# A sixteenth of layer 3's exponentials moved to VectorE, and the four attentions run as one stream

## The chip, the cores and the metric

The kernel runs on one core of a Trainium2 chip. A core has five engines, each with its own instruction stream that it works through in order: TensorE (PE, matrix products; its weight loads are listed as PEld), ScalarE (ACT, activations such as the exponential), VectorE (DVE, element-wise work), GpSimd (POOL) and SyncE (SP, which issues most DMAs). They meet through semaphores. The metric is the device time of one execution in microseconds. The kernel before takes 4205.69 us (median of three runs, 4199.02 to 4210.75).

## The reference, cut to what matters

Four layers follow each other on an input of 2 x 128 x 64 x 64, each of the form `x = x + layer(group_norm(x))`. Layer 3 is softmax attention over all 4096 positions, with 8 heads of 16 channels:

```python
q, k, v = proj(wq, bq), proj(wk, bk), proj(wv, bv)      # (B, 8, 16, 4096)
a = jnp.einsum('bhcq,bhck->bhqk', q, k) / jnp.sqrt(128.)
a = jax.nn.softmax(a, axis=-1)
o = jnp.einsum('bhqk,bhck->bhcq', a, v)
x = x + o.reshape(B, C, h, w)
```

Layer 0 has, among much else, one softmax attention with 4 heads of 32 channels over the same 4096 positions. Both attentions skip the maximum of the softmax (a bound on the scores is checked, with a general version behind it) and so need, for each score, one exponential, one product with the values, and a share in a sum.

## The kernel before, in words

The layers run one after the other. Everything in layers 0 and 3 is issued in the order of the program on each engine: `_in_order` ties each instruction to the one before it on its engine, so nothing is rearranged by a scheduler.

**Layer 3.** Each of the 2 batch entries has 2 groups of 4 heads, so there are four attentions. An attention takes its 4096 queries in 8 blocks of 512 (`qb`), and for each block its 4096 keys in 32 tiles of 128 (`kt`): 1024 iterations in all. One iteration does this:

- `scores` (L2102): 8 matmuls into two PSUM tiles `ps_s` of 128 x 1024, called here pair 0 and pair 1 (heads 0 and 1, heads 2 and 3). Query and key are each split in two parts, so each head has two matmuls that add up; all first parts are issued (two for pair 0, two for pair 1), then all second parts.
- two activations (L2112), one for each pair: the exponential of 128 x 1024 scores from PSUM to a `weights` tile in SBUF.
- `multiply` (L2121) for the iteration two before this one: 4 matmuls (8 records in the trace) that add weights times values to one accumulator `ps_acc`. Beside the values, `vt` holds a column block of ones, so the sum for the softmax is accumulated in the same product.

PSUM is full: the pool `f3_sp` has three tiles for scores and `f3_acc` two of half that size. Since an iteration takes two of three score tiles in rotation, pair 0 of an iteration reuses the tile of pair 1 two iterations before, and pair 1 reuses the tile of pair 0 of the iteration just before.

After the last key tile of a block, `done` divides by the sum: five DVE operations (L2143 to L2148; the reciprocal L2146 takes 128 x 512 elements), and four DMAs write the rows out.

The side work prepares the next attention while one runs: queries and keys (L2030 to L2046), values (L2056, L2063), the bound (L2076 to L2091), the statistics of the next batch entry. It is a generator that is advanced after the iterations kt = 4, 12 and 20 of each block. Its matmuls go between two iterations on TensorE. In the first block of the first attention it is advanced before every even iteration, since its keys and values are only just being made. Each attention ends by draining its last two `multiply` before the next starts.

**Layer 0's attention** (L1343, L1352, L1760, L1800) has the same tiling. There the softmax's sum is made otherwise: DVE adds the weights of several iterations (128 x 2048 elements each), and TensorE then reduces the result with a matrix of ones (4 matmuls). `SUMMED` says how many iterations go in one such group: 7, 6, 7, 6 and 6 of the 32.

Of the kernel before, what the change touches and what calls it, by code (L numbers as in the profile page):

```python
# [17 lines left out]
S = H * W  # L18
CH = 512
# [1268 lines left out]
SUMMED = (7, 6, 7, 6, 6)  # L1288
F32R = mybir.dt.float32r
ENGINES = (  # L1290
# [672 lines left out]
def _layer3(ctx, tc, X, l3, cst, out, worst, here):  # L1963
# [6 lines left out]
    pp = ctx.enter_context(tc.tile_pool(name="f3_p", bufs=8))  # L1970
# [16 lines left out]
    def folded(b, got):  # L1987

        x = X[:, b, :]
        if b:  # L1990
            mean, rstd = _group_stats_pow(nc, two, acc, x, cst, mhalf)
        else:
            mean, rstd = here[:, 0:1], here[:, 1:2]
        yield
# [24 lines left out]
    def queries_and_keys(b, t, f, q, k, idle):  # L2019

        wqk, _, bqk, _ = f
        bq, bk, bk2 = (bqk[:, n, t : t + 1] for n in range(3))
        for c in range(NCH):
            cols = slice(c * CH, (c + 1) * CH)
            ps = acc()
            nc.tensor.matmul(ps, wqk[:, t, :], X[:, b, cols], start=True, stop=True)  # L2030

            qq = two.tile([128, CH], F32, tag="qq", name="qq", bufs=1)
            nc.vector.stream_shuffle(qq, ps, OF_Q)  # L2033
            kk = two.tile([128, CH], F32, tag="kk", name="kk", bufs=1)
            nc.vector.stream_shuffle(kk, ps, OF_K)  # L2035
            hi = two.tile([128, CH], F32R, tag="hi", name="hi", bufs=1)
            if c < idle:
                nc.scalar.activation(hi, kk, AF.Identity, bias=bk)
                nc.scalar.activation(kk, kk, AF.Identity, bias=bk2, scale=upper)
                nc.scalar.activation(q[0][:, cols], qq, AF.Identity, bias=bq)  # L2040
            else:
                nc.vector.tensor_scalar_add(hi, kk, bk)
                nc.vector.tensor_scalar(kk, kk, bk, upper, ALU.add, ALU.mult)
                nc.vector.tensor_scalar_add(q[0][:, cols], qq, bq)
            nc.vector.scalar_tensor_tensor(k[:, cols], hi, sign, kk, ALU.mult, ALU.add)
            nc.vector.scalar_tensor_tensor(  # L2046
                q[1][:, cols], qq, bq, q[0][:, cols], ALU.add, ALU.subtract
            )
            yield
# [20 lines left out]
    def bound(b, t, q, k):  # L2070


        top = two.tile([128, 2, 2], F32, tag="top", name="top")
        for n, x in enumerate((q[0], k)):
            for i in range(2):
                nc.vector.tensor_reduce(  # L2076
                    top[:, n, i : i + 1],
                    x[:, i * S // 2 : (i + 1) * S // 2],
                    AX.X,
                    ALU.max,  # L2080
                    apply_absolute_value=True,
                )
                yield
        m = two.tile([128, 2], F32, tag="m", name="m")
        nc.vector.tensor_reduce(m, top, AX.X, ALU.max)
        mm = two.tile([128, 1], F32, tag="mm", name="mm")
        nc.vector.scalar_tensor_tensor(mm, m[:, 0:1], lower, m[:, 1:2], ALU.mult, ALU.mult)
        ps = acc()
        nc.tensor.matmul(ps[:, 0:1], head_sum, mm, start=True, stop=True)
        n = 1 + 2 * b + t  # L2090
        nc.vector.tensor_scalar_mul(worst[:, n : n + 1], ps[:, 0:1], 1.02)  # L2091
        yield

    def attend(b, t, q, k, vt, early):
        ac = [None]

        def scores(qb, kt):
            ps = [spp.tile([128, 2, CH], F32, tag="sp", name="ps_s") for _ in range(2)]
            for n in range(2):
                for j in range(4):  # L2100
                    rows = slice(32 * j, 32 * j + 32)
                    nc.tensor.matmul(  # L2102
                        ps[j // 2][:, j % 2, :],
                        k[rows, kt * 128 : (kt + 1) * 128],
                        q[n][rows, qb * CH : (qb + 1) * CH],
                        start=(n == 0),
                        stop=(n == 1),
                    )
            w = []
            for p in range(2):  # L2110
                w.append(pp.tile([128, 2, CH], F32, tag="weights", name="weights"))
                nc.scalar.activation(w[p], ps[p], AF.Exp)  # L2112
            return w

        def multiply(qb, kt, w):
            if kt == 0:
                ac[0] = acc()
            for j in range(4):

                i = j % 2  # L2120
                nc.tensor.matmul(  # L2121
                    ac[0][32 * j : 32 * j + 32, :],
                    vt[:, kt, j // 2, i : i + 2, :].rearrange("p a d -> p (a d)"),
                    w[j // 2][:, i, :],
                    start=(kt == 0),
                    stop=(kt == NQT - 1),
                )
            if kt == NQT - 1:
                done(qb, ac[0])

        def done(qb, ps):
            cols = slice(qb * CH, (qb + 1) * CH)

            places = [
                (slice(32 * j + 16 * (j % 2), 32 * j + 16 * (j % 2) + 16),
                 slice(64 * t + 16 * j, 64 * t + 16 * j + 16))
                for j in range(4)
            ]
            xs = residual[qb % 2]
            for to, rows in places:  # L2140
                nc.sync.dma_start(xs[to, :], X[rows, b, cols])
            u = two.tile([128, CH], F32, tag="u", name="u", bufs=1)
            nc.vector.tensor_copy(u, ps)  # L2143
            r = two.tile([128, CH], F32, tag="r", name="r", bufs=1)
            nc.vector.stream_shuffle(r, u, [(i + 16) % 32 for i in range(32)])  # L2145
            nc.vector.reciprocal(r, r)  # L2146
            nc.vector.tensor_mul(u, u, r)  # L2147
            nc.vector.tensor_add(u, u, xs)  # L2148
            for at, rows in places:
                nc.sync.dma_start(out[b, rows, cols], u[at, :])  # L2150

        waiting = []
        for qb in range(NCH):
            for kt in range(NQT):
                if kt % 2 == 0:
                    over = next(early, early) is early
                waiting.append((qb, kt, scores(qb, kt)))
                if len(waiting) > 2:
                    multiply(*waiting.pop(0))
                yield kt if over else None  # L2160
        for x in waiting:
            multiply(*x)
# [10 lines left out]
    def work():  # L2173

        for b in range(B):
            f = []
            yield from folded(b, f)
            for t in range(2):
                first = b == 0 and t == 0
# [12 lines left out]
                else:  # L2192
                    for _ in early:
                        yield
# [155 lines left out]
```

## Time and profile before

One profiled execution took 4197.72 us; its span, from first to last instruction, is 4195.9 us. The median of the timed runs is 8 us above the former.

| stretch of the profiled execution | us |
|---|---|
| layer 0's two attentions, first to last exponential (L1352) | 193 to 803 and 1003 to 1590 |
| layer 3's attention, start of the first to start of the last exponential (L2112) | 2234.3 to 4179.7 |
| end of the span | 4195.9 |
| ACT busy with L2112 | 1884.8 (2048 instructions) |
| ACT idle before L2112 | 62.8 |
| granted TensorE clock, mean | 0.985 |

In a line of the profile, the operation is followed by what it writes and reads, its shape and count; after the bar stand the busy time in us, the mean duration of one in ns, and the idle time of the engine before these instructions with what ended it. Instructions of one engine overlap, so the busy time over the count is closer to the pace than the mean duration is.

### The profile page before, as it was taken

How to read it: one execution, taken by the hardware profiler on the slowest of the kernel's cores; microseconds unless marked ns; L12 is line 12 of the kernel's file. 1: busy time of each engine (PE TensorE's matmuls, PEld its weight loads, DVE VectorE, ACT ScalarE, POOL GpSimd, SP SyncE). 2: the span in 40 equal slices, each digit the busy share in tenths (PEclk: the TensorE clock that was granted, in tenths of full speed). 3: DMA queues.
4: the chain of work that ended last, by engine and by line, in shares of the span. 5: the costliest groups of instructions: out<-in, count | busy, mean ns of one | idle time of the engine just before them, and what ended most of it. 6: DMA issues, size and time to landing. Idle time of an engine off the chain costs nothing. (4 is left out here: it accounts for less than half of the span.)

```text
span 4195.9 us, 90633 instructions
## 1 busy us (share of the span) xinstructions
PE 4026.9 (96%) x40014; PEld 1494.0 (36%) x40014; DVE 2127.8 (51%) x2374; ACT 3332.9 (79%) x4035; POOL 71.3 (2%) x145
## 2 busy tenths in 40 slices
PE   7999999989999998997999999999999999999998
PEld 4522222354222224445664333333333333333332
DVE  4678888657888888986754112221132102211111
ACT  4478888735888883326647999999999999999998
POOL 1001000010000001000000000000000000000000
PEclk9999999999999999998999999999999999999999
DMA  1199960000000000004750000000000000000000
GB/s 49 29 188 182 179 90 1 2 2 2 2 1 2 2 1 12 1 1 171 290 208 4 6 6 6 4 6 6 4 6 6 6 4 6 6 4 6 6 6 5
DMA packets 158855, 159.40 MB, mean 38 GB/s; under 512 B 24809, under 2 KB 148713, under 8 KB 154354
## 3 DMA queue, kind: packets, MB, share of 16 engines
q1 hardware_dynamic: 158450, 153.50, 15.7%
q8 instruction: 315, 5.16, 0.5%
q14 instruction: 90, 0.74, 0.1%
HBM read 145.09 MB, written 73.40 MB: 52 GB/s over the span
## 5 line engine op out<-in xcount | busy, mean ns | idle before, releaser
L2112 ACT ACTIVATE weights<-ps_s 128x1024 f32<-128x1024 f32 x2048 | 1884.8, 1099 | 62.8 <-PE ps_s L2102 62.3
L1352 ACT ACTIVATE weights<-ps_s 128x1024 f32<-128x1024 f32 x1024 | 992.9, 1023 | 180.6 <-PE ps_s L1343 164.2
L2121 PE MATMUL ps_acc<-weights,vt 128*32 128x512 f32 x8192 | 1092.8, 605 | 0.0
L2102 PE MATMUL ps_s<-q,k 32*128 32x512 f32 x8192 | 924.9, 444 | 5.4 <-ACT weights L2112 5.4
L1800 DVE TENSOR_TENSOR sums<-sums,weights 128x2048 f32<-128x2048 f32 x352 | 806.7, 2292 | 38.4 <-ACT weights L1352 5.2
L2102 PEld LDWEIGHTS ps_s<-q,k 32*128 32x128 f32 x8192 | 471.2, 182 | 839.4 <-ACT weights L2112 773.6
L1343 PE MATMUL ps_s<-q,k 32*64 32x512 f32 x8192 | 627.3, 613 | 7.1 <-ACT weights L1352 2.4
L1760 PE MATMUL ps_acc<-weights,vt 128*32 128x512 f32 x4096 | 550.9, 606 | 6.6 <-ACT weights L1352 3.6
L2143 DVE COPY u<-ps_acc 128x512 f32<-128x512 f32 x32 | 22.1, 691 | 1039.0 <-PE ps_acc L2121 1039.0
L1343 PEld LDWEIGHTS ps_s<-q,k 32*64 32x64 f32 x8192 | 159.6, 130 | 436.4 <-PE ps_s L1343 320.3
L2121 PEld LDWEIGHTS ps_acc<-weights,vt 128*32 128x32 f32 x8192 | 162.9, 108 | 379.2 <-issue 367.2
L1800 DVE TENSOR_TENSOR sums<-weights 128x2048 f32<-128x2048 f32 x80 | 183.3, 2291 | 113.6 <-ACT weights L1352 113.6
L1760 PEld LDWEIGHTS ps_acc<-weights,vt 128*32 128x32 f32 x4096 | 81.2, 108 | 426.3 <-issue 403.3
L662 DVE SCALAR_TENSOR_TENSOR X<-g,w,X 128x2048 f32<-128x2048 f32 x84 | 197.4, 2350 | 2.6
L1548 PE MATMUL ps_sp<-pad,diag 32*32 32x512 f32 x4608 | 158.9, 597 | 2.3 <-ACT q L1568 1.3
L1008 PE MATMUL ps_z<-w_ri,e 128*32 128x128 f32 x2048 | 137.3, 408 | 14.3 <-DVE e L950 12.1
L2063 DVE TENSOR_TENSOR vt<-ps_acc,bv 128x384 f32<-128x384 f32 x32 | 17.8, 557 | 246.0 <-PE ps_acc L2056 246.0
L1548 PEld LDWEIGHTS ps_sp<-pad,diag 32*32 32x32 f32 x4608 | 95.0, 103 | 54.2 <-issue 15.9
L2033 DVE LOAD_MASK_SELECT qq<-ps_acc x32 | 0.4, 14 | 222.6 <-PE ps_acc L2030 222.6
L2146 DVE RECIPROCAL r<-r 128x512 f32<-128x512 f32 x32 | 107.3, 3353 | 1.1
L950 DVE TENSOR_SCALAR e<-ps_pe 32x136 f32<-32x136 f32 (+1 forms) x352 | 104.4, 297 | 4.9
L948 ACT ACTIVATE e<-ps_pe 32x136 f32<-32x136 f32 (+1 forms) x352 | 99.2, 282 | 4.1
(289 smaller groups left out, 2552.5 us busy)
## 6 DMA issues: line engine op xcount, KB each, us to landing
w_ri<-w_r SPq DMA_DIRECT2D x16, 2112.0 KB, 8.2
w_ri<-w_i SPq DMA_DIRECT2D x16, 2112.0 KB, 13.5
w_r<-in_L_conv_kr_w SPq DMA_DIRECT2D x15, 528.0 KB, 13.5
w_r<-in_L_conv_kr_x SPq DMA_DIRECT2D x15, 528.0 KB, 13.3
w_r<-in_L_conv_kr_y SPq DMA_DIRECT2D x15, 528.0 KB, 13.0
w_r<-in_L_conv_kr_z SPq DMA_DIRECT2D x15, 528.0 KB, 13.2
w_i<-in_L_conv_ki_w SPq DMA_DIRECT2D x15, 528.0 KB, 13.8
w_i<-in_L_conv_ki_x SPq DMA_DIRECT2D x15, 528.0 KB, 12.7
```

The costliest lines, as they stand in the source:

```text
L662: nc.vector.scalar_tensor_tensor(xi, g[:, i : i + H // 2, j : j + W], w8[:, s : s + 1], xi, ALU.mult, ALU.add)
L950: nc.vector.tensor_scalar_mul(out, got[of, :, s], sign)
L1008: nc.tensor.matmul(out.rearrange("p (n f o) -> p n f o", n=2, f=2), e[:, s, 2 * j : 2 * j + 2, :].rearrange("p f x -> p (f x)"), w.rearran ...
L1343: nc.tensor.matmul(ps[j // 2][to, j % 2, :], k[rows, kt * 128 + 64 * half : kt * 128 + 64 * half + 64], q[rows, qb * CH : (qb + 1) * CH], ...
L1352: nc.scalar.activation(w[:, 2 * p : 2 * p + 2, :], ps[p], AF.Exp)
L1548: nc.tensor.matmul(ps[r // 2][to, r % 2, :].rearrange("p (h w) -> p h w", w=W), diag[rows, grp, t, :], pad[rows, y0 : y0 + ROWS, t % 3 : t ...
L1760: nc.tensor.matmul(ac[n][rows, :], lhs(rows), w[:, j, :], start=first, stop=last)
L1800: nc.vector.tensor_add(parts[0].rearrange("p j c -> p (j c)"), t.rearrange("p j c -> p (j c)"), w.rearrange("p j c -> p (j c)"),)
L2102: nc.tensor.matmul(ps[j // 2][:, j % 2, :], k[rows, kt * 128 : (kt + 1) * 128], q[n][rows, qb * CH : (qb + 1) * CH], start=(n == 0), stop= ...
L2112: nc.scalar.activation(w[p], ps[p], AF.Exp)
L2121: nc.tensor.matmul(ac[0][32 * j : 32 * j + 32, :], vt[:, kt, j // 2, i : i + 2, :].rearrange("p a d -> p (a d)"), w[j // 2][:, i, :], star ...
L2146: nc.vector.reciprocal(r, r)
```

## The change

In layer 3, four of the 64 exponentials of a block are taken from ACT and computed on DVE: pair 0 of the key tiles 4 and 18, pair 1 of 11 and 25. DVE scales and converts a score to an integer, whose bits are taken apart into an exponent and a mantissa, evaluates a polynomial in the mantissa, and multiplies by the power of two: eight instructions on 128 x 1024 elements, where the first reads PSUM and so gives the score tile back. The first is issued with the scores, the others in six steps, one before each following iteration. The finished weights are multiplied later, in the places 10, 17, 24 and 31 of the order of products (`ORDER`). `LAG` is now 3 iterations instead of 2, and there are 12 tiles for weights instead of 8.

Queries are kept in a tile for each block of 512 rather than one for all. The side work is cut into smaller steps and placed after the iterations in `SIDE`: a block of keys and queries is spread over four of them (only the first has a matmul), and values, bound and statistics use the others. The maxima for the bound are taken with each block of keys (128 x 512) rather than later over 128 x 2048. `done` transposes the accumulator, takes four reciprocals of 32 x 16 elements, multiplies, and transposes back. The four attentions share one list of products that wait, so that none drains before the next.

In layer 0, `SUMMED` becomes four groups of eight.

```diff
-SUMMED = (7, 6, 7, 6, 6)
+SUMMED = (8, 8, 8, 8)
...
+LAG = 3
+SIDE = (6, 9, 13, 16, 20, 23, 27, 30)
+BY_VECTOR = {(4, 0): 10, (11, 1): 17, (18, 0): 24, (25, 1): 31}
...
-    pp = ctx.enter_context(tc.tile_pool(name="f3_p", bufs=8))
+    pp = ctx.enter_context(tc.tile_pool(name="f3_p", bufs=12))
     spp = ctx.enter_context(tc.tile_pool(name="f3_sp", bufs=3, space=PSUM))
...
+    def exponentials(ps, out):
+        i = two.tile([128, 2 * CH], I32, tag="exp_i", name="exp_i", bufs=1)
+        nc.vector.tensor_scalar(
+            i, ps.rearrange("p j c -> p (j c)"), EXP_SCALE, EXP_BIAS, ALU.mult, ALU.add
+        )
+        yield
+        m = two.tile([128, 2 * CH], I32, tag="exp_m", name="exp_m", bufs=1)
+        nc.vector.tensor_scalar(
+            m, i, 0x7FFFFF, 0x3E800000, ALU.bitwise_and, ALU.bitwise_or
+        )
+        nc.vector.tensor_scalar(
+            i, i, 0x7F800000, 0x40000000, ALU.bitwise_and, ALU.bitwise_xor
+        )
+        yield
+        m, power = m.bitcast(F32), i.bitcast(F32)
+        z = two.tile([128, 2 * CH], F32, tag="exp_z", name="exp_z", bufs=1)
+        x = m
+        for n in EXP_TERMS[:-1]:
+            nc.vector.scalar_tensor_tensor(z, x, n, m, ALU.add, ALU.mult)
+            x = z
+            yield
+        w = pp.tile([128, 2, CH], F32, tag="weights", name="weights")
+        nc.vector.scalar_tensor_tensor(
+            w.rearrange("p j c -> p (j c)"), z, EXP_TERMS[-1], power, ALU.add, ALU.mult
+        )
+        out.append(w)
+        yield
...
+        for p in range(2):
+            g.weights[qb, kt, p] = w = []
+            if (kt, p) in BY_VECTOR:
+                chain[0] = exponentials(ps[p], w)
+                next(chain[0])
+            else:
                 w.append(pp.tile([128, 2, CH], F32, tag="weights", name="weights"))
-                nc.scalar.activation(w[p], ps[p], AF.Exp)
+                nc.scalar.activation(w[0], ps[p], AF.Exp)
...
-            u = two.tile([128, CH], F32, tag="u", name="u", bufs=1)
-            nc.vector.tensor_copy(u, ps)
-            r = two.tile([128, CH], F32, tag="r", name="r", bufs=1)
-            nc.vector.stream_shuffle(r, u, [(i + 16) % 32 for i in range(32)])
-            nc.vector.reciprocal(r, r)
-            nc.vector.tensor_mul(u, u, r)
-            nc.vector.tensor_add(u, u, xs)
+        z = two.tile([128, CH // 32, 32], F32, tag="z", name="z", bufs=1)
+        flat = z.rearrange("p n i -> p (n i)")
+        nc.vector.transpose(flat, ps)
+        r = two.tile([128, CH // 32], F32, tag="r", name="r")
+        for j in range(4):
+            rows = slice(32 * j, 32 * j + 32)
+            nc.vector.reciprocal(r[rows, :], z[rows, :, 16 * (1 - j % 2)])
+        nc.vector.tensor_mul(z, z, r.unsqueeze(2).to_broadcast([128, CH // 32, 32]))
+        u = two.tile([128, CH], F32, tag="u", name="u", bufs=1)
+        nc.vector.transpose(u, flat)
+        nc.vector.tensor_add(u, u, xs)
...
+        for n in range(NCH * NQT):
+            qb, kt = divmod(n, NQT)
+            if kt % 2 == 0:
+                over = next(early, early) is early
+            next(chain[0], None)
+            scores(g, qb, kt)
+            waiting.append((g, qb, kt))
+            if len(waiting) > LAG:
+                multiply(*waiting.pop(0))
+            if not over or kt not in SIDE:
+                continue
+            at = SIDE.index(kt)
+            if qb == 0 or following is None:
+                next(others, None)
+                continue
+            if after is None:
+                run(others)
+                after, others = following()
+            if at % 2 == 0:
+                next(after.keys[qb - 1])
+            else:
+                next(others, None)
```

In the first block of the first attention, `early` is `in_turn(in_pieces(chained(*g.keys[2:]), 4), g.values)`: before every even iteration it issues either all four steps of a block of keys or one step of values, as before.

## The prediction

> **What bounds the kernel now.** I read the chain first. TensorE carries it, and nearly half the span is layer 3.
>
> ```profile
> PE 47%; DVE 1%; ACT 0%; issue 0%; DVEq 0%; ACTq 0%
> ```
>
> The groups contradict it.
>
> ```profile
> L2112 ACT ACTIVATE weights<-ps_s 128x1024 f32<-128x1024 f32 x2048 | 1884.8, 1099 | 62.8 <-PE ps_s L2102 62.3
> L2121 PE MATMUL ps_acc<-weights,vt 128*32 128x512 f32 x8192 | 1092.8, 605 | 0.0
> L2102 PE MATMUL ps_s<-q,k 32*128 32x512 f32 x8192 | 924.9, 444 | 5.4 <-ACT weights L2112 5.4
> ```
>
> From 2234 to 4180 us ACT idles for 63 us of 1946. So I took a stretch with no side work, 3900 to 4150 us, by groups and by waits:
>
> ```profile
> L2112 ACT ACTIVATE weights<-ps_s 128x1024 f32<-128x1024 f32 x274 | 251.4, 1118 | 0.0
> ...
> PEld ps_s L2102 <- ACT weights L2112: 114.0, 136, 0.8
> ```
>
> ACT never idles; 251.4 us over 274 is 0.917 each, 1.833 an iteration. Whether TensorE could go faster is seen where it was late, in the timeline about one step of side work:
>
> ```profile
> 2952.28 1.13 PE L2056 MATMUL ps_acc<-wv,X 128*128 128x96 f32 x8
> 2953.34 0.74 PE L2102 MATMUL ps_s<-q,k 32*128 32x512 f32 x8
> 2954.01 1.07 PE L2121 MATMUL ps_acc<-weights,vt 128*32 128x512 f32 x8
> 2954.18 5.61 ACT L2112 ACTIVATE weights<-ps_s 128x1024 f32<-128x1024 f32 x6 [0.86 <-PE ps_s L2102]
> 2955.01 0.98 PE L2102 MATMUL ps_s<-q,k 32*128 32x512 f32 x8
> 2956.91 0.91 PE L2102 MATMUL ps_s<-q,k 32*128 32x512 f32 x8
> ```
>
> The side matmuls hold the scores up for 1.06 (2952.28 to 2953.34), ACT idles; then scores follow scores after 1.67 (2953.34 to 2955.01), then 1.90. So TensorE alone needs 1.67 an iteration and waits 0.17 in an ordinary one. Two short windows show where: the first has four score matmuls begun at once, the second, an ordinary iteration, only two.
>
> ```profile
> 2953.34 0.51 PE L2102 MATMUL ps_s<-q,k 32*128 32x512 f32 x4
> ...
> 2956.91 0.49 PE L2102 MATMUL ps_s<-q,k 32*128 32x512 f32 x2
> ```
>
> Pair 1 waits for the PSUM tile of pair 0 of the iteration before. This closes a loop. From the single records, with B the start of pair 1's first score matmul: the tile is free 0.05 after the exponential's end; the second parts of pair 0 start 0.16 after B; a ready ACT ends that exponential 1.52 after those. Together 1.73, against ACT's own 1.83. TensorE is never further ahead than three tiles allow, so slack is 0.10 an iteration, and a side step of 1.06 costs 0.95: 64 of them make ACT's 62 us.
>
> **What the Trainium skill says.** "PSUM — Partial Sum Buffer", Specifications, gives eight banks of 512 fp32 values: three score tiles of two and two accumulators of one fill it, so no fourth tile exists. "VectorE: DVE Perf Modes", The perf-mode tier table: fp32 from PSUM runs at one element a cycle and a tensor-scalar in SBUF at two; the trace agrees on the first (a copy of 128x1024 from PSUM, below, takes 1.225). Same page, Two Vector instructions with no wait between them: one whose start quadrant differs from the last one's waits until it has finished. No row here shows that for reciprocals. The rows I price by (groups, one tile's instructions, and the timeline at the end of a block):
>
> ```profile
> L1559 DVE COPY tok<-ps_sp 128x1024 f32<-128x1024 f32 x5 | 6.1, 1225 | 18.8 <-PE ps_sp L1610 18.8
> ...
> L1775 DVE RECIPROCAL rec<-by_query x16: 225/253/256, 294.6 to 1595.7; 128x16 f32<-128x16 f32 x16
> ...
> 2608.47 0.91 PE L2102 MATMUL ps_s<-q,k 32*128 32x512 f32 x8
> 2608.61 0.69 DVE L2143 COPY u<-ps_acc 128x512 f32<-128x512 f32 x1 [19.55 <-PE ps_acc L2121]
> ```
>
> **The change, part by part.** Sums are against the profiled span of 4195.9 (4197.72 in all).
>
> *The exponentials removed.* 128 leave ACT, 117 us of its time. But ACT cannot use it: after it skips one, its next input is not there. If pair 1 is skipped (kt 11, 25), ACT ends pair 0, and the next exponential ends 1.73 later instead of 1.83: −0.10 each. If pair 0 is skipped (kt 4, 18), DVE's first operation frees the tile. It is ready 0.16+0.39+0.05=0.60 after B, takes 1.22 (the copy's row) and 0.05 to signal: the next B comes at 1.87 instead of 1.83, +0.04, and 0.10 is won after it: −0.06.
>
> *DVE late at kt=4.* The products of a block's last tile now follow the scores of kt=2 of the next block, so `done` starts 0.14 after the scores of kt=3 begin (2608.47 to 2608.61 above). It stands in DVE's queue ahead of the first operation of kt=4. Its length: transpose 0.75 (row L1773, 0.71, and 0.035 between dependent instructions), four reciprocals of 0.253+0.03 (held by quadrant) 1.13, product 0.73, transpose 0.75, sum 0.60 until the next independent instruction starts: 3.95. Pair 0 of kt=4 is ready 1.83+0.78=2.61 after the scores of kt=3 begin. DVE comes at 0.14+3.95=4.09, 1.48 late. TensorE stands at pair 1 of kt=5 for that long, products behind it too, and ACT has only pair 1 of kt=4 to do. With the 0.04 and the 0.10: +1.42. Between the bounds: were the reciprocals overlapped, 0.3 less.
>
> A block: 1.42−0.06−0.20=+1.16. Of 32 blocks, 31 have a `done` in front: +36.
>
> *First block.* Keys are made there as they are used. DVE has, from the first scores to the first operation of kt=18: five blocks of keys at 6.1 (1.49+1.51+1.49+1.38 for two maxima, from rows L2033 to L2046 and a maximum of 512 at 0.69 scaled from L2076, plus gaps), 30; five of values at 0.6, 3; two chains; that first operation, 1.3; and 4.5 left from keys before. A chain is 1.22, two bit operations of 0.69 (price of the same table: 1024/2 cycles and the fixed part), five of 1.25 (L2046's 0.746 for 512, plus 512 elements at 1.04 ns), gaps 0.3: 9.2. Sum 57. Scores of kt=19 wait for it; before they start 45.7 after the first ones. The least is +12; DVE also waits for TensorE's key matmuls in turn, so I take +18, between 12 and 26. If bit operations run at one element a cycle, +2.
>
> *First blocks of the other three attentions:* two operations of 0.75 for the last keys stand before kt=4's: +1.5 each, +4.5.
>
> *Side steps.* As many matmuls as before, each still 0.95 (none lies in the iteration of an exponential removed): 0. Maxima, keys and chains fit between: about 48 of 60 us of a block on DVE. The chain's length is hidden by the later places and the 12 tiles of weights: it ends some 7 iterations after it starts, its product comes after 9. LAG 3 adds a third product to the last drain, which runs under ACT's last exponentials: 0. SP issues the same eight DMAs a block in the same order; the loads of a block go out behind the stores of the block before, some 50 us ahead of their use: 0.
>
> *One stream.* At each of three ends ACT loses about 2 us to the drain, and 2.5 more at one where TensorE's clock halved: −8.5. *Start:* two maxima ahead of the first scores, +1.3. *End:* the last `done` takes 4.0 instead of 6.36 (4181.94 to 4188.30): −2.3.
>
> Layer 3: 36+18+4.5−8.5+1.3−2.3=+49.
>
> *Layer 0.* TensorE sets the pace there (scores to scores 2.04, and 2.90 with a sum's four ones matmuls). 16 of 80 sums go: −0.86x16=−14. DVE adds once more per block,
>
> ```profile
> L1800 DVE TENSOR_TENSOR sums<-sums,weights 128x2048 f32<-128x2048 f32 x351 | 804.4, 2292 | 38.3 <-ACT weights L1352 5.2 <-DVE sums L1800 0.5
> ```
>
> 2.40 with its gap: 28 of them and 2.4 for the division are 69.6 of 71.6 us, hidden by TensorE, but no longer in the blocks with side work, some five: −10, between −14 and +5.
>
> Together +39; TensorE's clock, below, +5: 4195.9+44 is 4240 for the profiled execution. The median lies 8 us above it before, so 4205.69+44=4250.
>
> **The rivals.** *A, faster:* ACT's time is what counts and offloading shortens it. For it: ACT idle is 0 in the quiet stretch. Against: the loop of 1.73. All 117 gone, −10 for layer 0, −9.5 for one stream, start and end, +18 for the first block: 4087. It decides if the next scores stand ready when ACT skips, that is, if the gap between ACT's ends there is 0.92 rather than 1.7. *B, same:* DVE is at kt=4 in time, since `done` is shorter or starts earlier. Then 31x1.48=46 fall away: 4204. Point: `done` below 2.5 us. *C, much slower:* the skill ("TensorE: Matmul & The Clock Gate", The HAM clock gate) halves the clock after an idle window of 3.4 us. Here one window with TensorE busy 2.11 us of 3.40 is followed by 6.8 us at 0.5, and at another attention's end 5.46 of 7.00 is not (columns: length, busy of PE, PEld, DVE, ACT, POOL with counts, clock, DMA):
>
> ```profile
> 3220.80:3224.20 3.40, 2.11 (x18) 0.87 (x18) 3.30 (x4) 2.66 (x3) 0.00 (x0) 1.00 0.00 0
> 3224.20:3231.00 6.80, 6.55 (x34) 1.91 (x38) 6.73 (x5) 4.99 (x6) 0.00 (x0) 0.50 0.13 31
> 2727.00:2734.00 7.00, 5.46 (x46) 1.94 (x45) 3.86 (x4) 5.13 (x7) 0.00 (x0) 1.00 0.01 4
> ```
>
>  A stall of 1.7 leaves such a window at about 0.55 to 0.6 where it falls inside whole, half the time. Each costs 1.6; in all 32 blocks +51, 4296; I counted three.
>
> **Chances.** Main 0.72; A 0.08; B 0.10; C 0.10. Main alone: 4225 to 4280, from the first block's ±7, layer 0's and the reciprocals. B and part of C inside leave 4208 to 4300. A run tells about 0.3% from no change, 12.6 us. Faster: A and a fifth of B, 0.10; same 0.08; slower 0.82.
>
> **What would show it.** In the profile after: first operation on `exp_i` at kt=4 starting some 1.5 us after its scores end, scores to scores 3.3 to 3.4 there once a block; ACT idle before L2167 (the exponential's new line) near 230 us, not 63; TensorE's weight loads waiting for DVE; a block without side work at 59.8 us against 58.65; 16 fewer sums in layer 0. I am wrong if ACT's total idle stays near 60, if `done` ends before kt=4's scores, or if ACT's pace itself changes with DVE reading PSUM beside it.

## The result and the profile after

The kernel takes 4225.45 us with the change (median of six runs, 4219.93 to 4229.62) against 4207.64 us before (median of six, 4199.02 to 4210.75): a ratio of 1.0044, 95% interval 1.0033 to 1.0056. It is slower, by 18 us where 44 were forecast. The profiled execution took 4224.26 us, with a span of 4222.5.

From the page of the kernel after, the chain of work that ended last by engine, and four of the costliest groups (after the bar: busy us, mean ns of one, and the idle time of the engine before them with what ended it):

```profile
PE 41%; DVE 6%; issue 0%; ACT 0%; DMA 0%; POOL 0%; SPq 0%; POOLq 0%; DVEq 0%
...
L2167 ACT ACTIVATE weights<-ps_s 128x1024 f32<-128x1024 f32 x1920 | 1782.9, 1066 | 194.5 <-PE ps_s L2153 194.3
...
L2153 PE MATMUL ps_s<-q,k 32*128 32x512 f32 x8192 | 915.7, 443 | 40.7 <-DVE exp_i L2109 39.2
...
L2109 DVE TENSOR_SCALAR exp_i<-ps_s 128x1024 int32<-128x1024 f32 x128 | 156.5, 1223 | 217.7 <-PE ps_s L2153 217.4
...
L1827 DVE TENSOR_TENSOR sums<-weights 128x2048 f32<-128x2048 f32 x64 | 146.6, 2291 | 62.4 <-ACT weights L1379 62.0
```

ACT lost 102 us of busy time (1884.8 to 1782.9) and gained 132 of idle time (62.8 to 194.5). Busy plus idle went from 1947.6 to 1977.4, and that difference, 30 us, is what layer 3 lost: the work taken off ACT turned into waiting for scores, and then some. VectorE, 1% of the chain before, is 6% of it now, and TensorE's score matmuls, which waited 5.4 us for ACT in the whole run, wait 39.2 for VectorE's first operation.

Where a block loses it is seen in the timeline of the kernel after, at kt = 3 to 6 of a block without side work (columns: start, length, engine, line, operation, names, shapes, count, idle time before):

```profile
3855.56 0.91 PE L2153 MATMUL ps_s<-q,k 32*128 32x512 f32 x8
3855.70 0.72 DVE L2199 STREAM_TRANSPOSE z<-ps_acc 128x512 f32<-128x512 f32 x1 [8.41 <-PE ps_acc L2176]
...
3856.45 1.02 DVE L2203 RECIPROCAL r<-z 32x16 f32<-32x16 f32 x4
...
3857.40 0.91 PE L2153 MATMUL ps_s<-q,k 32*128 32x512 f32 x8
...
3859.23 0.50 PE L2153 MATMUL ps_s<-q,k 32*128 32x512 f32 x2
3859.59 1.22 DVE L2109 TENSOR_SCALAR exp_i<-ps_s 128x1024 int32<-128x1024 f32 x1
...
3860.86 0.73 PE L2153 MATMUL ps_s<-q,k 32*128 32x512 f32 x6 [1.13 <-DVE exp_i L2109]
...
3861.47 2.85 ACT L2167 ACTIVATE weights<-ps_s 128x1024 f32<-128x1024 f32 x3 [2.11 <-PE ps_s L2153]
...
3862.52 0.77 PE L2153 MATMUL ps_s<-q,k 32*128 32x512 f32 x8
```

`done` starts at 3855.70, 0.14 after the scores of kt = 3, and VectorE comes to kt = 4 (scores at 3857.40) only at 3859.59. TensorE has begun pair 0 of kt = 5 at 3859.23 and can't begin pair 1 before 3860.86; ACT idles 2.11. From the scores of kt = 5 to those of kt = 6 (3859.23 to 3862.52) it is 3.29 instead of 1.83; this is called the stall at kt = 4 below, after the exponential that causes it.

The starts of the scores give layer 3 block by block (us, the two profiled executions):

| blocks | before | after | change | forecast |
|---|---|---|---|---|
| the first | 68.6 | 79.2 | +10.7 | +18 |
| first of the other three attentions | 178.4 | 181.3 | +2.9 | +5.5 |
| last of three attentions, before with the drain | 187.0 | 184.9 | -2.1 | -2.5 |
| the other 25 | 1510.9 | 1529.1 | +18.2 | +29.0 |
| all | 1944.9 | 1974.5 | +29.6 | +50 |

(The forecast's terms by block: 1.16 for each but the very first, 4.5 more for the second row, and of the 8.5 for the drains 2.5 in the second row, where the clock had halved, and 6 in the third.)

Layer 0's two stretches, first to last exponential, went from 609.3 to 603.4 and from 587.2 to 580.7: -12.4, with the 64 groups of sums that the last line above counts, where there were 80. With +0.75 ahead of layer 3's first exponential and -1.4 behind its last that makes +17, where the medians differ by 18. The two profiled spans differ by 26.5: in the execution after the change the parts that it doesn't touch took some 9 us longer. (The profiled execution before lay 10 us below its median, the one after 1.)

### The profile page after: what moved, and what is told of

It is laid out like the page before. It is cut to its first block, busy times and chain, and to the rows that moved or that the text cites. A ratio compares the mean times of both kernels' runs of the same rounds, so it can differ in the third digit from the quotient of the medians.

```text
span 4222.5 us, 90716 instructions
## 1 busy us (share of the span) xinstructions
PE 4015.2 (95%) x39886; PEld 1480.3 (35%) x39886; DVE 3179.2 (75%) x3526; ACT 3231.0 (77%) x3907; POOL 74.5 (2%) x145
## 5 line engine op out<-in xcount | busy, mean ns | idle before, releaser
L2167 ACT ACTIVATE weights<-ps_s 128x1024 f32<-128x1024 f32 x1920 | 1782.9, 1066 | 194.5 <-PE ps_s L2153 194.3
L1379 ACT ACTIVATE weights<-ps_s 128x1024 f32<-128x1024 f32 x1024 | 993.1, 1023 | 169.4 <-PE ps_s L1370 151.2
L2153 PE MATMUL ps_s<-q,k 32*128 32x512 f32 x8192 | 915.7, 443 | 40.7 <-DVE exp_i L2109 39.2
L1827 DVE TENSOR_TENSOR sums<-sums,weights 128x2048 f32<-128x2048 f32 x384 | 880.0, 2292 | 44.2 <-ACT weights L1379 7.8
L2153 PEld LDWEIGHTS ps_s<-q,k 32*128 32x128 f32 x8192 | 454.2, 182 | 884.1 <-ACT weights L2167 704.2
L2125 DVE SCALAR_TENSOR_TENSOR exp_z<-exp_z,exp_m 128x1024 f32<-128x1024 f32 x384 | 469.6, 1223 | 10.1
L2109 DVE TENSOR_SCALAR exp_i<-ps_s 128x1024 int32<-128x1024 f32 x128 | 156.5, 1223 | 217.7 <-PE ps_s L2153 217.4
L1827 DVE TENSOR_TENSOR sums<-weights 128x2048 f32<-128x2048 f32 x64 | 146.6, 2291 | 62.4 <-ACT weights L1379 62.0
L2199 DVE STREAM_TRANSPOSE z<-ps_acc 128x512 f32<-128x512 f32 x32 | 22.9, 716 | 217.4 <-PE ps_acc L2176 217.4
L2129 DVE SCALAR_TENSOR_TENSOR weights<-exp_z,exp_i 128x1024 f32<-128x1024 f32 x128 | 156.4, 1222 | 11.4 <-ACT weights L2167 0.5
L2125 DVE SCALAR_TENSOR_TENSOR exp_z<-exp_m 128x1024 f32<-128x1024 f32 x128 | 156.0, 1219 | 0.0
L1008 PE MATMUL ps_z<-w_ri,e 128*32 128x128 f32 x2048 | 137.5, 409 | 14.5 <-DVE e L950 12.4
L1575 PEld LDWEIGHTS ps_sp<-pad,diag 32*32 32x32 f32 x4608 | 95.1, 103 | 55.7 <-issue 17.1
```

The source lines that it names most:

```text
L1379: nc.scalar.activation(w[:, 2 * p : 2 * p + 2, :], ps[p], AF.Exp)
L1575: nc.tensor.matmul(ps[r // 2][to, r % 2, :].rearrange("p (h w) -> p h w", w=W), diag[rows, grp, t, :], pad[rows, y0 : y0 + ROWS, t % 3 : t ...
L1827: nc.vector.tensor_add(parts[0].rearrange("p j c -> p (j c)"), t.rearrange("p j c -> p (j c)"), w.rearrange("p j c -> p (j c)"),)
L2109: nc.vector.tensor_scalar(i, ps.rearrange("p j c -> p (j c)"), EXP_SCALE, EXP_BIAS, ALU.mult, ALU.add)
L2125: nc.vector.scalar_tensor_tensor(z, x, n, m, ALU.add, ALU.mult)
L2129: nc.vector.scalar_tensor_tensor(w.rearrange("p j c -> p (j c)"), z, EXP_TERMS[-1], power, ALU.add, ALU.mult)
```

## The experiments

Below, "the stretch" is layer 3 from its first to its last exponential on ACT: 1945.5 us before, 1975.5 after. "A quiet block" has no side work: 58.7 before, 59.6 after. The theory is that of the prediction: the loop of score tiles gives ACT at most 0.10 us for an exponential removed, and VectorE, late at kt = 4, holds up TensorE. Its rivals: ACT's work counts (A), and VectorE slows ACT merely by reading PSUM beside it (D, the last sentence of the prediction).

**All exponentials back on ACT.**

```diff
-BY_VECTOR = {(4, 0): 10, (11, 1): 17, (18, 0): 24, (25, 1): 31}
+BY_VECTOR = {}
```

> No exponential goes to VectorE; all else is as in the changed kernel. Theory S (score tiles: ACT cannot use the time it is spared, because TensorE is held by three score tiles; the stall at kt=4 and the first block are the loss): the 0.96 us a block measured in quiet blocks, times 31, and the first block's 10.7 go away, so the stretch from first to last exponential of layer 3 falls from 1975.5 to about 1935, and the time to about 4185. Rival A (ACT's time is what counts): giving 117 us of work back to ACT makes it slower than the changed kernel, some 4340. Rival D (VectorE's work beside ACT and TensorE slows them): also about 4185, so A alone is told apart here, D by the next two.

Measured: 4183.0 us (4181.42 to 4188.04), ratio to the kernel before 0.9948 (0.9935 to 0.9962), stretch 1938.5, quiet block 58.66. Everything else in the change, taken together, is a gain, of 24 us against the 4206.97 that the kernel before took beside this run; the exponentials on VectorE cost 42 us. In the page of this kernel ACT's group reads

```profile
L2167 ACT ACTIVATE weights<-ps_s 128x1024 f32<-128x1024 f32 x2048 | 1884.6, 1104 | 56.5 <-PE ps_s L2153 55.9
```

with 57 us of idle time, not 195.

**The same four exponentials a block, all of pair 1.**

```diff
-BY_VECTOR = {(4, 0): 10, (11, 1): 17, (18, 0): 24, (25, 1): 31}
+BY_VECTOR = {(4, 1): 10, (11, 1): 17, (18, 1): 24, (25, 1): 31}
```

> As many exponentials on VectorE (key tiles 4, 11, 18, 25), but all four of pair 1, whose score tile is wanted again one step later. Theory S: no stall at kt=4, since VectorE has until the scores of kt=6; each of the four makes its iteration 1.68 instead of 1.83, so 0.62 a block less than with none: stretch about 1915 to 1918, time about 4167. Rival D (VectorE's work itself slows the others): as slow as the changed kernel, 4225, since VectorE does as much. Rival A: the gain would be much larger than 0.15 each.

Measured: 4185.18 us (4183.09 to 4191.25), ratio 0.9956 (0.9942 to 0.9969), stretch 1934.8, quiet block 58.25. VectorE does exactly the work of the changed kernel, in the same iterations, and the time is 40 us shorter: D falls, and what costs is which pair is taken at kt = 4, where `done` stands in front. The timeline of a quiet block, from the scores of kt = 4 to those of kt = 6:

```profile
3884.95 0.91 PE L2153 MATMUL ps_s<-q,k 32*128 32x512 f32 x8
...
3886.79 0.91 PE L2153 MATMUL ps_s<-q,k 32*128 32x512 f32 x8
3887.14 1.22 DVE L2109 TENSOR_SCALAR exp_i<-ps_s 128x1024 int32<-128x1024 f32 x1
...
3888.63 0.80 PE L2153 MATMUL ps_s<-q,k 32*128 32x512 f32 x8
```

VectorE comes to kt = 4 exactly as late as in the changed kernel, 2.19 after its scores (3884.95 to 3887.14). But its tile is wanted only for kt = 6, and these scores start 1.84 after those of kt = 5. Lateness alone does no harm, then: it takes a late VectorE and a tile that TensorE needs next. A falls too: 117 us less for ACT and no gain against e1_none. A quiet block gains 0.41, four times 0.10: the iteration after an exponential of pair 1 takes 1.73 here, as the prediction's loop has it. The 1.68 that I had read from the changed kernel, and expected here, occurs only where an exponential of pair 0 was taken before it (1.67 in e3_done_later too, where VectorE isn't late); why is open. The gain is spent in the first blocks: 75.95 us in the very first against 69.44 where nothing is taken there (e7_cut_pair1 below), and +1.3 in each of the other three.

**`done` behind the scores of kt = 4.**

```diff
-            done(g.b, g.t, qb, g.ac)
+            ended.append((g.b, g.t, qb, g.ac))
...
             scores(g, qb, kt)
+            while ended and kt == 4:
+                done(*ended.pop())
```

> The division at the end of a block is issued after the scores of the next block's kt=4, so that VectorE takes the first step of that exponential before it. The same instructions otherwise. Theory S: the stall of 1.46 at kt=4 becomes 0.04, 28 blocks of it, and in part at three more: stretch 1975.5 less about 42, 1933; time about 4183. Rival D: no change, 4225.

Measured: 4191.84 us (4189.0 to 4199.5), ratio 0.9966 (0.9952 to 0.9979), stretch 1944.9. The same place in a quiet block, from the scores of kt = 4 to those of kt = 6:

```profile
3899.58 0.91 PE L2153 MATMUL ps_s<-q,k 32*128 32x512 f32 x8
3900.36 1.22 DVE L2109 TENSOR_SCALAR exp_i<-ps_s 128x1024 int32<-128x1024 f32 x1 [10.88 <-PE ps_s L2153]
...
3901.41 0.96 PE L2153 MATMUL ps_s<-q,k 32*128 32x512 f32 x8
3901.50 0.70 DVE L2199 STREAM_TRANSPOSE z<-ps_acc 128x512 f32<-128x512 f32 x1
...
3903.30 0.77 PE L2153 MATMUL ps_s<-q,k 32*128 32x512 f32 x8
```

VectorE takes the exponential 0.78 after its scores, and `done` follows. The stall is gone (1.88 instead of 3.29) and a quiet block takes 58.18. Pair 0 is taken as in the changed kernel, and is no loss when VectorE is there in time, so the lateness is shown to be the cause. Twelve of the expected us are missing in the stretch. Its execution, of 4199.5 us, was the slowest of the five; in the median 9 are missing. The first blocks of the other three attentions take 62.3 to 64.7: there TensorE now waits for VectorE's step of the bound, which stands behind the last keys and the exponential (2.72 us in one of them, in an iteration of 5.1), and the clock halves behind that wait (20.5 us of half clock in this execution's layer 3, 3.4 in that of after).

**`done` 0.75 us longer**, its first transposition issued twice.

```diff
         nc.vector.transpose(flat, ps)
+        nc.vector.transpose(flat, ps)
```

> The division is made 0.75 longer by a transpose done twice. If the lateness of VectorE alone counts, each block loses 0.75 more: stretch about 1999, time about 4249. But in this program the score tile that waits for VectorE is another one: the program's order of waits shows pair 0 of kt=6 in 31 blocks, where the changed kernel has pair 1 of kt=5 in 28. If that assignment counts, TensorE is held only until the first operation ends, some 2.4 from scores to scores instead of 3.29: stretch about 1952, time about 4202, that is, faster for a longer division.

Measured: 4202.71 us (13 runs, 4195.75 to 4210.06), ratio 0.999 (0.9982 to 0.9998), stretch 1955.2, quiet block 58.68. A longer `done` makes the kernel 23 us *faster*, as the second half of the expectation had it. The timeline of this kernel at the same place (the scores of kt = 3, 4, 5 and 6):

```profile
3839.37 0.91 PE L2153 MATMUL ps_s<-q,k 32*128 32x512 f32 x8
...
3841.20 0.91 PE L2153 MATMUL ps_s<-q,k 32*128 32x512 f32 x8
...
3843.03 0.92 PE L2153 MATMUL ps_s<-q,k 32*128 32x512 f32 x8
...
3844.14 1.22 DVE L2109 TENSOR_SCALAR exp_i<-ps_s 128x1024 int32<-128x1024 f32 x1
...
3845.41 0.50 PE L2153 MATMUL ps_s<-q,k 32*128 32x512 f32 x4 [0.46 <-DVE exp_i L2109]
```

VectorE begins later, 2.94 after the scores of kt = 4 instead of 2.19, and yet kt = 5 is begun whole at 3843.03; only kt = 6 waits, and for 0.46. In the waits that the program writes out, the first matmul to wait for VectorE's tile is pair 0 of kt = 6 in 31 blocks here; after the change it is pair 1 of kt = 5 in 28 blocks, pair 0 of kt = 6 in the first blocks of the other three attentions, and pair 0 of kt = 7 in the very first. A score tile doesn't go round in fixed order, as the kernel before had led me to assume: whoever needs a tile next doesn't always get the one read late. What the pool goes by was not tried.

**Layer 0's groups back.**

```diff
-SUMMED = (8, 8, 8, 8)
+SUMMED = (7, 6, 7, 6, 6)
```

> The changed kernel with SUMMED = (7, 6, 7, 6, 6) again, nothing else. If the gain of layer 0 comes from the sixteen sums saved: layer 0's two stretches (first to last exponential) go back from 603 and 581 us to 609 and 587, layer 3's stretch stays at 1975, and the time is 4225 + 12 = 4238. If layer 0 gained for another reason, such as the different execution: 603 and 581 stay, 4225.

Measured: 4238.69 us (4234.03 to 4240.69), ratio 1.0065 (1.0051 to 1.0078); layer 0's stretches 608.5 and 587.2, layer 3's 1976.8. The sixteen sums are worth 13 us by the medians and 11.6 by the two stretches of layer 0. (The kernel before, too, took 3 us more beside this run than beside the changed kernel, so 13 is rather too much.)

**Can the side work hide in the slack?** The next kernels were built on e1_none, to test the 0.10 us from another side: a side step costs 0.95, so its matmuls in pieces might vanish. In e6_cut a step's matmuls are quarters, one after each iteration: keys and queries behind kt = 4 to 10, values behind kt = 11 to 30. `g.cut` is true for the three later attentions.

```diff
-        nc.tensor.matmul(ps, wqk[:, t, :], X[:, b, cols], start=True, stop=True)
+        if g.cut and c < NCH - 1:
+            for i in range(4):
+                nc.tensor.matmul(
+                    ps[:, i * 128 : (i + 1) * 128],
+                    wqk[:, t, :],
+                    X[:, b, c * CH + i * 128 : c * CH + (i + 1) * 128],
+                    start=True,
+                    stop=True,
+                )
+                if i < 3:
+                    yield
+        else:
+            nc.tensor.matmul(ps, wqk[:, t, :], X[:, b, cols], start=True, stop=True)
```

The four tiles of a step of values are parted in the same way. e7_cut_pair1 adds the four exponentials of pair 1, but not in the first blocks (the edit is shown with e11_best), and e8_cut_best moves the first attention's maxima behind its keys:

```diff
-        for n, x in enumerate((q[c][0], k[:, cols])):
-            nc.vector.tensor_reduce(
-                top[:, n, c : c + 1], x, AX.X, ALU.max, apply_absolute_value=True
-            )
+        if g.cut:
+            maxima(g, c)
         yield
...
     def bound(g):
+        if not g.cut:
+            for c in range(NCH):
+                maxima(g, c)
+                yield
```

> All exponentials on ScalarE, the rest of the change, and the side matmuls of the three later attentions cut into quarters, one quarter after each iteration (keys and queries: four pieces of 128 columns; values: one of four tiles). The slack theory: a piece of 0.27 us fits into the 0.17 that TensorE waits in an iteration and the 0.10 of slack in the loop, so some 45 side steps of 0.95 us vanish: layer 3's stretch 1938 - 43 = 1895, time near 4140, and ScalarE idles some 20 us in all before its exponentials. The rival, that TensorE's work is what counts and each piece costs its length: no gain, 1935 to 1940, 4183.

> As e6_cut, with four exponentials of pair 1 on VectorE in each block but the first of each attention. Slack theory: -0.10 us for each of 112, so 11 less than e6_cut, if the iterations concerned carry no piece of side work; where they carry one, the slack is spent already and the gain is less or turns into a loss of up to 0.17 each. Between 1884 and 1895, time near 4130 to 4140. The rival, that ScalarE's time counts once the side work is hidden: 112 x 0.917 = 103 less than e6_cut.

> As e7_cut_pair1, but the first attention's maxima are not taken with each block of keys in its first block: they follow after all keys, from kt = 24 on. If the maxima, ahead of the next copies of keys in VectorE's queue, make the first block 4 us longer: first block near 69 instead of 73, 4 less than e7_cut_pair1. If something else in the change does: no difference.

Measured: e6_cut 4188.8 us (4184.94 to 4189.39), ratio 0.9946 (0.9932 to 0.9959), stretch 1939.6; e7_cut_pair1 4191.19 (4187.31 to 4198.73), 0.996 (0.9947 to 0.9974), 1943.9; e8_cut_best 4196.8 (4187.81 to 4197.14), 0.9963 (0.9949 to 0.9976), 1942.7. Cutting gains nothing: with a quarter of keys after each of four iterations, scores follow scores after 2.25 once and then three times after 2.08, which is the 1.67 of TensorE alone and 0.41 for a quarter, where a fourth of a whole step would be 0.27. In e7_cut_pair1 an exponential of pair 1 in a quiet block still gives 0.10. But at kt = 11 VectorE stands behind the steps of the keys, and in most blocks that have them the iteration after takes 2.71 instead of 1.83 (3.31 in one). The stretch is 4.3 longer than e6_cut's although its first block is 3.4 shorter: a loss in place of the 11 us, and nothing like 103.

The maxima explain only 1.0 of the 4 us that I put on them: the first block takes 69.44 in e7_cut_pair1, 68.44 in e8_cut_best. (The medians, 5.6 us the other way, can't show it: e8_cut_best's five runs lie at 4188 and at 4197, and its profile is of one at 4188.6.) The rest of what had made me suspect them (72.84 in e1_none) is TensorE's clock. The same 17.1 us around the first scores, first in e1_none, then in e7_cut_pair1 (columns: window, its length, busy time of PE, PEld, DVE, ACT and POOL with counts, granted clock, DMA share and GB/s):

```profile
2222.40:2239.50 17.10, 15.18 (x64) 7.41 (x64) 10.51 (x23) 9.88 (x11) 0.00 (x0) 0.50 0.00 1
```

```profile
2225.90:2243.00 17.10, 14.67 (x122) 6.10 (x118) 13.68 (x28) 13.83 (x15) 0.00 (x0) 1.00 0.00 1
```

At half clock TensorE does 64 matmuls where it does 122 at full clock, and the block is 3.4 us longer.

**Pieces at a distance.** As e6_cut, but at most one after every second iteration: keys in eighths, values in quarters. (e10_spaced_pair1 adds the edits of e7_cut_pair1 and e8_cut_best.)

```diff
-            if 4 <= kt < 11:
+            if kt in (4, 6, 8, 10, 12, 14, 16, 18, 19, 21, 23):
                 next(after.keys[qb - 1])
-            elif 11 <= kt < 31:
+            elif kt in (20, 22, 24, 26) or (qb, kt) == (1, 28):
                 next(others, None)
```

> As e1_none, but the side matmuls of the three later attentions are cut and set after every second iteration at most: keys and queries in eighths of 64 columns, values in quarters. In e6_cut a quarter lengthened an iteration that had no wait left by 0.41 us (2.08 against 1.67), which is 0.15 more than a quarter of a whole step, and with a piece in every iteration nothing can be regained. Slack theory: TensorE can be 0.17 + 0.10 = 0.27 late in an iteration at no cost, if the next iteration is free to regain it. An eighth, about 0.41 - 0.13 = 0.28, then costs 0.01 to 0.02, a quarter 0.14; two iterations of TensorE with an eighth need 3.62 of 3.66. Three attentions: 21 steps of keys from 0.95 to 0.1, 21 of values from 0.95 to 0.56 (three stay whole): -26, layer 3's stretch near 1913, time near 4158. The rival, that a piece costs its whole length wherever it stands: 21 x (8 x 0.28 - 0.95) + 21 x (4 x 0.41 - 0.95) = +42, stretch near 1980, time near 4225.

> As e9_spaced, with four exponentials of pair 1 on VectorE in each block but the first of each attention, and the first attention's maxima taken after all keys. Slack theory: 28 quiet blocks at -0.40 would be -11, but in the 21 blocks with pieces the iterations concerned (5, 12, 19 and 26) have spent the slack that the gain consists of, or VectorE comes late behind the keys' own steps, so -3 (the last attention's seven blocks) to -11, and -1 for the maxima: stretch 4 to 12 less than e9_spaced. If ScalarE's time counts now that the side work is hidden: up to 112 x 0.917 = 103 less.

Measured: e9_spaced 4213.19 us (21 runs, 4209.81 to 4217.8), ratio 1.0012 (1.0005 to 1.0018), stretch 1964.6; e10_spaced_pair1 4208.73 (4201.14 to 4216.21), 1.0 (0.9992 to 1.0009), 1961.9. So e9_spaced's stretch is 26 us longer than e1_none's where I expected it 26 shorter. e10_spaced_pair1's is 2.7 shorter than that of e9_spaced although 2.9 longer in the first block (72.38 against 69.44, with 13.7 us of half clock around its start): the exponentials of pair 1 give some 6 us, within the 4 to 12 expected and far from 103. The timeline of e9_spaced about two eighths of keys:

```profile
2373.74 0.43 PE L2051 MATMUL ps_acc<-X,wqk 128*128 128x64 f32 x2
...
2374.10 0.74 PE L2168 MATMUL ps_s<-q,k 32*128 32x512 f32 x8
...
2374.93 3.77 ACT L2182 ACTIVATE weights<-ps_s 128x1024 f32<-128x1024 f32 x4 [0.16 <-PE ps_s L2168]
...
2375.77 0.97 PE L2168 MATMUL ps_s<-q,k 32*128 32x512 f32 x8
...
2377.66 0.43 PE L2051 MATMUL ps_acc<-X,wqk 128*128 128x64 f32 x2
```

An eighth holds the scores up for 0.36 (2373.74 to 2374.10), and one of these pairs of iterations takes 3.93 instead of 3.67: +0.26. So only 0.10 of a piece is hidden, as of a whole step (1.06, of which 0.95 shows). My 0.27 added the 0.17 that TensorE waits before pair 1, which is no slack: with the wait, the second parts of pair 0 start 0.17 + 0.16 after the first score matmul; without it, behind four first parts begun at once, they start 0.33 after it. The next exponential's input comes at the same time either way. A piece costs its length less 0.10, and a short piece is long for its size: 0.36 for 64 columns of keys, 0.41 for a quarter of keys, 0.39 for one of values, 1.06 for a whole step. Put into the sum, 21 steps of keys at 8 x 0.26 and 21 of values at 4 x 0.29, each instead of 0.95, are +28; less the 3.4 of e1_none's clock, 25 of the measured 26. That explanation was made after the run; it uses the measured piece, but the slack of 0.10 is the prediction's own.

**Only what gains.** e2_pair1 without VectorE's exponentials in the first block of each attention, and the first attention's maxima behind its keys.

```diff
-            if (kt, p) in BY_VECTOR:
+            if qb and (kt, p) in BY_VECTOR:
...
-            i, kt = j % 2, ORDER[j // 2][at]
+            i, kt = j % 2, ORDER[j // 2][at] if qb else at
```

> As e2_pair1, but no exponential on VectorE in the first block of each attention, and the first attention's maxima taken after all keys. If e2_pair1 lost its gain in those four blocks (75.95 us against 69.44 in the very first, and some 1.3 in each of three others), the stretch of layer 3 is 1934.8 - 6.5 - 1.0 - 4 = 1923, and the time 4173 to 4175. If the gain is lost elsewhere, the stretch stays near 1933 and the time near 4184.

Measured: 4172.97 us (4170.62 to 4180.0), ratio to the kernel before 0.9915 (0.9902 to 0.9929), stretch 1928.7. This beats both kernels, the changed one by 52 us. Of the stretch, 4.2 lie in the first block (72.63, with 17.1 us of half clock around its start, against 68.44 in e8_cut_best) and 1.7 in the second, where TensorE once waits for VectorE's step of the bound; without them it is 1923, as expected. From its page:

```profile
L2176 ACT ACTIVATE weights<-ps_s 128x1024 f32<-128x1024 f32 x1936 | 1794.0, 1072 | 137.2 <-PE ps_s L2162 136.7
```

Even here 112 exponentials fewer give about 10 us: against e1_none's, ACT's busy time fell by 91 and its idle time grew by 81.

## Where the prediction held, and which of its steps failed

The direction and the mechanism hold. e1_none, e2_pair1 and e3_done_later each take the stall away in another manner, and each is 34 to 42 us faster than the changed kernel; in the latter two VectorE has as many exponentials as in the changed kernel. The size was wrong: +18 measured, +44 forecast. Of the 27 us between the forecast and the +17 of the profiles, the first block makes 7, VectorE's exponentials in the other blocks 10 (5 in the 25 of the table, 4 in the first blocks of the other three attentions), the clock 5, the side steps and layer 0 somewhat over 2 each. So two steps of the prediction failed, the first block's sum and the rule of which matmul waits, and two more terms were too large: the stall's size and the clock's.

- *Failed step: the sum for the first block.* Its least was +12, its forecast +18, and it was +10.7. The 57 us for VectorE up to the first operation of kt = 18 were 51.0. I had put a gap between instructions that don't depend on each other, where they overlap (two maxima of 0.68 start 0.59 apart). The offloaded exponentials cost 9.8 there (79.24 against 69.44), the maxima 1.0. Nor is it the one wait that the sum was made for: the iteration that waits for kt = 18's tile is 5.8 longer (a wait of 4.0, and 3.4 us of half clock behind it), and four others are 0.4 to 1.5 longer each.
- *Failed step: which matmul waits.* I let pair 1 of kt = 5 reuse VectorE's tile in every block. In the first blocks of the other three attentions it is another tile, and there, where 2.7 each were forecast for the exponentials, they cost 1.2 (181.3 against 177.6 in e1_none, over three). e4_done_longer shows how much hangs on it: 0.9 a block. That 28 blocks did wait as forecast was luck in this respect: the rule that I had used isn't the one by which tiles are given out.
- *VectorE late at kt = 4.* From the start of `done` to VectorE's next operation 3.89 (forecast 3.95); late by 1.42 (1.48); net with the iteration behind it +1.32 (+1.42). Of "VectorE: DVE Perf Modes" in the Trainium skill, both points used hold in the trace: four reciprocals on four quadrants start 0.255 apart at 0.245 each (Two Vector instructions with no wait between them), and a bit operation of 1024 elements takes 0.695 against 1.223 for one that reads PSUM (The perf-mode tier table).
- *The exponentials removed.* Pair 0 at kt = 18: -0.05 (forecast -0.06). Pair 1 at kt = 11 and 25: -0.155 each (forecast -0.10), but exactly -0.10 where no pair 0 is taken before them (e2_pair1). ACT gets nothing of its 117 us.
- *A block*: +0.93 in place of +1.16, from the two terms above; over 25 blocks 6 us.
- *Side steps*, costed as unchanged: they cost 2.3 less, by e1_none against the kernel before, both without the first block and the drains. Where this comes from is open. The 25 blocks of the table are 5.4 shorter, the first and last of the attentions 3 longer, since some of the steps have moved into these.
- *One stream*: the drains had cost 8.9 (three last iterations of 3.91 instead of 1.83, and 2.7 of half clock in the block behind one; forecast 8.5), and they are gone. *Start and end*: +0.75 and -1.4 (forecast +1.3 and -2.3).
- *Layer 0*: -12.4 in the profile (forecast -10, with a bound of -14 where VectorE's added work is hidden throughout).
- *The clock*: +5 forecast, nothing seen. One window of 3.4 us at half clock in layer 3, in the first block's stall; before, 6.8 us. The 28 stalls of 1.4 us at kt = 4 didn't halve it, so rival C fell. A fell with e2_pair1 and e11_best. B didn't happen, as `done` took 3.9, not under 2.5.

## What to carry to other kernels

An engine that never idles may still not be the one to unload: look at what its next input waits for. If that is a buffer which the engine itself gives back, work taken off it turns into waiting, and only the small difference between the loop and the engine's own pace is won. Before work moves to another engine's queue, write down what stands in that queue at that moment, and which of the next buffers is held until then; in e4_done_longer the second outweighed 0.75 us more in front of every block.

## What the runs showed beyond the prediction

- Making VectorE's division 0.75 us longer made the kernel 23 us faster, because the program was then laid out with another tile for the next scores: its waits, read before the run, gave 4202 us, and 4202.7 were measured.
- A short fp32 matmul set between the score matmuls isn't short: 64 columns of keys hold TensorE up for 0.36, 512 for about 1.06.
- Where TensorE starts again after a nearly idle window (0.64 of 3.40 us busy in e1_none, 0.33 of 3.50 in e7_cut_pair1), its clock is halved. In e7_cut_pair1 the next window was busy throughout and the clock came back after 3.4 us; in e1_none it stayed at half for 17.1 us, of which TensorE was busy 15.18. The Trainium skill ("TensorE: Matmul & The Clock Gate", The HAM clock gate) has the full clock return after one busy window of about 3.4 us, with which the first agrees and the second doesn't. Of the five windows in e1_none's 17.1 us, the third was busy throughout as well, and the clock came back only behind the fifth (columns as in the windows above):

```profile
2229.20:2232.60 3.40, 3.40 (x18) 2.57 (x22) 3.33 (x8) 2.58 (x3) 0.00 (x0) 0.50 0.00 0
...
2236.00:2239.50 3.50, 3.50 (x14) 0.56 (x6) 0.00 (x0) 1.21 (x2) 0.00 (x0) 0.51 0.00 0
```

The other three were busy 2.71 to 2.87 of 3.40. (e6_cut and e11_best show the same five windows.) The ends of matmuls are modelled in the profile, so a busy window may hold gaps that it doesn't show. What decides wasn't settled; the same first block took 69.44 or 72.84 us for it.
